# A selective-scan loop in another layout: one state on 128 channels a unit in place of four states on 32 channels

## The chip, the cores and the metric

The kernel runs on one core of one Trainium2 chip. The metric is the device time of one execution in microseconds (us). In the profile the engines are PE (TensorE matmuls), PEld (TensorE weight loads), DVE (VectorE), ACT (ScalarE), POOL (GpSimd) and SP (SyncE, which only issues transfers here). Each engine works through its own queue in order; a semaphore wait at the head of a queue holds back everything behind it.

## The reference

Four images of 192 x 64 x 64 pass through four layers, all in f32. Only the first two matter here:

- Layer 0: a layer norm over the 192 channels, then two Mamba blocks side by side (the second sees the channels reversed), and `xs + y1 + y2`.
- Layer 1: a layer norm, one Mamba block, a 3x3 depthwise convolution with batch norm and gelu, another layer norm, and an MLP of 768 hidden channels.
- Layers 2 and 3: a dynamic 3x3 convolution and a sedenion (16-component) window product with an MLP.

The core of a Mamba block, for 384 inner channels d, 16 states n and 4,096 positions t:

```
dt = softplus(dt @ dt_w.T + dt_b)
A  = -exp(A_log)
h[d,n] = exp(dt[d] * A[d,n]) * h[d,n] + (dt[d] * x[d]) * B[n]     # along t
y[d]   = sum over n of h[d,n] * C[n]   + D[d] * x[d]
y = y * silu(z)
```

So for every pair (d, n) there is a first-order recurrence along 4,096 positions, with a factor, an input and a weighted sum over n around it.

## The kernel before, in words

The program is three stages, one after the other: `two_mambas` (layer 0), `mamba_block` (layer 1) and `conv_and_windows` (layers 2 and 3, not touched). The last one starts when the first two have ended.

A Mamba block is traced by two pieces. `Mamba.front` (L240) makes the inputs of the scan for 512 positions (T): projection, a causal convolution as matmuls with diagonal matrices, silu, the small projection to B, C and dt (`dbl`), softplus of dt, and `dtx = dt*xc`. It writes dt, dtx, xc, z and B/C to DRAM (`keep`). I call one Mamba block on one tile of 512 positions a round: 64 rounds in layer 0 (4 images x 8 tiles x 2 blocks), 32 in layer 1.

The class `Scan` (L321) then works in units. A unit is a tile of 128 partitions that hold 32 channels x 4 states, and 1,024 elements a partition: in layer 0 one group of channels on 1,024 positions (P = 1, S = 4 units make 128 channels), in layer 1 two groups on 512 positions (P = 2, S = 2). There are 2,304 units. For each:

- `load` (L344), six units ahead: dt and dtx come from DRAM with each channel's row repeated on four partitions (L354), B and C with four rows repeated for 32 channels (L359), on SP's queue;
- `inputs` (L365), two units ahead: `w = dtx * B` on POOL (L369), into a pool of S + 3 buffers;
- `decay` (L373), one unit ahead: `dA = exp(dt * A)` on ACT, written to PSUM (L376), 2 buffers;
- `run` (L381): the scan on DVE (L388), in place in dA, or into w in one unit of four; ACT saves the last column as the state (L396); `w = h * C` on DVE reading PSUM, or in that one unit of four on POOL (L398);
- `add_up` (L400): when the S units of 128 channels are done, PE sums over states. Each matmul multiplies by a 128 x 32 selection matrix (`sel`) and writes 32 of the 128 output partitions of ps_y (L420). The skip term `D*x` is a matmul with a diagonal matrix into the same sum (L407);
- `gate` (L429): `y = ps_y * z` on DVE, reading PSUM (L433).

`Scan.stream` writes this order out by hand. Between units it takes steps of the `Background` queue (one a unit in layer 0, two in layer 1), in which the next tile's `front` and the work behind the last tile (`back`, `tail`) are cut up by `yield`. In these generators a matmul stands one step ahead of the ACT instruction that reads its result. A scheduler of the framework then fixes each engine's order when the program is built; it stays close to this one. An f32 matmul appears in the profile as two PE records.

Of the kernel before, what the change touches and what calls it, by code (L numbers as in the profile page):

```python
# [33 lines left out]
NJ = DI // 32  # L34
NQ = NS // 4
UW = 1024
# [172 lines left out]
class Mamba:  # L209
# [3 lines left out]
    def __init__(self, nc, name, taps, ins, const, work, psum, ident):  # L213
        self.nc, self.name, self.taps = nc, name, taps
        self.work, self.psum = work, psum
# [8 lines left out]
        self.conv_b, self.dt_b = w["conv_b"], w["dt_b"]  # L224
        self.x_w, self.out_w = w["x_w"], w["out_w"]
        self.A = const.tile([128, NQ, NJ], F32, name=f"{name}_A")
# [3 lines left out]
        self.D = const.tile([128, ND, 128], F32, name=f"{name}_D")  # L230
        for d in range(ND):
            for j in range(taps):
                nc.vector.tensor_scalar_mul(
                    self.conv[:, d, j, :], ident, w["conv_w"][:, d, j : j + 1]
                )
            nc.vector.tensor_scalar_mul(self.D[:, d, :], ident, w["D"][:, d : d + 1])
        self.halo = const.tile([128, ND, taps - 1], F32, name=f"{name}_halo")
        self.state = const.tile([128, NQ, NJ], F32, name=f"{name}_state")

    def front(self, xn, first, kept, at):  # L240

        nc, K = self.nc, self.taps
        cols = slice(at, at + T)

        def keep(name, t):
            nc.sync.dma_start(kept[name].rearrange("(d p) t -> p d t", p=128)[:, :, cols], t)

        raw = self.work.tile([128, ND, K - 1 + T], F32, name="raw", tag="raw", bufs=1)
        if first:
            nc.gpsimd.memset(raw[:, :, 0 : K - 1], 0.0)  # L250
        else:
            nc.gpsimd.tensor_copy(raw[:, :, 0 : K - 1], self.halo)
        z = self.work.tile([128, ND, T], F32, name="z", bufs=1)

        def project(e):
            ps = self.psum.tile([128, T], F32, name="ps_in", tag="mm")
            for k in range(2):
                nc.tensor.matmul(  # L258
                    ps, self.in_w[:, k, bass.ts(e, 128)], xn[:, k, :], start=(k == 0), stop=(k == 1)
                )  # L260
            return ps

        ps = project(0)
        for e in range(2 * ND):
            after = project(e + 1) if e + 1 < 2 * ND else None
            yield
            nc.scalar.copy(raw[:, e, K - 1 :] if e < ND else z[:, e - ND, :], ps)
            ps = after
        nc.gpsimd.tensor_copy(self.halo, raw[:, :, T:])
        xc = self.work.tile([128, ND, T], F32, name="xc", bufs=1)  # L270

        def convolve(d):
# [5 lines left out]
            return ps  # L278

        ps = convolve(0)  # L280
        for d in range(ND):
            after = convolve(d + 1) if d + 1 < ND else None
            yield
            nc.scalar.activation(xc[:, d, :], ps, AF.Identity, bias=self.conv_b[:, d : d + 1])  # L284
            ps = after
        nc.scalar.activation(xc, xc, AF.Silu)
        nc.scalar.activation(z, z, AF.Silu)
        keep("xc", xc)
        keep("z", z)
        yield  # L290
        ps = self.psum.tile([RK + 2 * NS, T], F32, name="ps_x", tag="mm")
        for d in range(ND):
            nc.tensor.matmul(ps, self.x_w[:, d, :], xc[:, d, :], start=(d == 0), stop=(d == ND - 1))
        yield
        dbl = self.work.tile([RK + 2 * NS, T], F32, name="dbl", bufs=1)
        nc.scalar.copy(dbl, ps)
        nc.sync.dma_start(kept["bc"][:, cols], dbl[RK:, :])
        dt = self.work.tile([128, ND, T], F32, name="dt", bufs=1)
        dtx = self.work.tile([128, ND, K - 1 + T], F32, name="dtx", tag="raw", bufs=1)[:, :, 0:T]

        def step_size(d):
            ps = self.psum.tile([128, T], F32, name="ps_dt", tag="mm")
            nc.tensor.matmul(ps, self.dt_w[:, bass.ts(d, 128)], dbl[:RK, :], start=True, stop=True)
            return ps

        ps, after = step_size(0), step_size(1)
        yield
        for d in range(ND):
            nc.scalar.activation(dt[:, d, :], ps, AF.Softplus, bias=self.dt_b[:, d : d + 1])  # L309
            ps, after = after, step_size(d + 2) if d + 2 < ND else None  # L310
        keep("dt", dt)
        yield
        for d in range(ND):
            nc.gpsimd.tensor_tensor(dtx[:, d, :], dt[:, d, :], xc[:, d, :], ALU.mult)
            if d < ND - 1:
                yield
        keep("dtx", dtx)
        yield


class Scan:  # L321

    AHEAD = 6

    def __init__(self, nc, ts, const, work, dram, psum_a, psum_y, ident):
        self.nc, self.ts, self.P, self.S = nc, ts, UW // ts, 4 * ts // UW  # L330
        self.work, self.dram, self.psum_a, self.psum_y = work, dram, psum_a, psum_y
        self.sel = const.tile([128, 32], F32, name="sel")
        nc.vector.tensor_reduce(
            self.sel, ident.rearrange("p (m n) -> p m n", n=4), AX.X, ALU.add
        )

    def block(self, mamba, first):
        kept = {
            n: self.dram.tile([rows, self.ts], F32, name=f"k_{n}")
            for n, rows in (("dt", DI), ("dtx", DI), ("xc", DI), ("z", DI), ("bc", 2 * NS))  # L340
        }
        return {"m": mamba, "first": first, "kept": kept, "used": {}}

    def load(self, u):  # L344
        nc, ts, P, S = self.nc, self.ts, self.P, self.S
        blk, c, q, s = u
        kept, used = blk["kept"], blk["used"]
        if q == 0:
            for n in ("dt", "dtx"):
                t = used[n, c, s] = self.work.tile([128, P, ts], F32, name=f"u_{n}", bufs=S + 1)  # L350
                for p in range(P):
                    j = 4 * c + s * P + p
                    rows = kept[n][bass.ts(j, 32), :]
                    nc.sync.dma_start(t[:, p, :], rows.unsqueeze(1).broadcast_to([32, 4, ts]))  # L354
        if s == 0:
            for n, r in (("B", 0), ("C", NS)):
                t = used[n, c, q] = self.work.tile([128, ts], F32, name=f"u_{n}", bufs=P + 1)
                rows = kept["bc"][r + 4 * q : r + 4 * q + 4, :]
                nc.sync.dma_start(t, rows.unsqueeze(0).broadcast_to([32, 4, ts]))  # L359
        if s == S - 1 and q in (0, 1):  # L360
            n = ("xc", "z")[q]
            t = used[n, c] = self.work.tile([128, ts], F32, name=f"u_{n}", bufs=1)
            nc.sync.dma_start(t, kept[n][bass.ts(c, 128), :])

    def inputs(self, u):  # L365
        blk, c, q, s = u
        blk["w", c, q, s] = w = self.work.tile([128, self.P, self.ts], F32, name="w", bufs=self.S + 3)
        b = blk["used"]["B", c, q].unsqueeze(1).broadcast_to([128, self.P, self.ts])
        self.nc.gpsimd.tensor_tensor(w, blk["used"]["dtx", c, s], b, ALU.mult)  # L369

    def decay(self, u):
        blk, c, q, s = u
        a = blk["a", c, q, s] = self.psum_a.tile([128, self.P, self.ts], F32, name="dA")  # L373
        for p in range(self.P):
            j = 4 * c + s * self.P + p
            self.nc.scalar.activation(  # L376
                a[:, p, :], blk["used"]["dt", c, s][:, p, :], AF.Exp, scale=blk["m"].A[:, q, j : j + 1]
            )

    def run(self, u, on_pool):  # L380
        nc, P = self.nc, self.P  # L381
        blk, c, q, s = u
        a, w = blk.pop(("a", c, q, s)), blk["w", c, q, s]
        h = w if on_pool else a
        j = 4 * c + s * P
        state = blk["m"].state[:, q, j : j + P]
        for p in range(P):
            nc.vector.tensor_tensor_scan(  # L388
                h[:, p, :],
                a[:, p, :],  # L390
                w[:, p, :],
                0.0 if blk["first"] else state[:, p : p + 1],
                ALU.mult,
                ALU.add,
            )
        nc.scalar.copy(state, h[:, :, self.ts - 1])  # L396
        cc = blk["used"]["C", c, q].unsqueeze(1).broadcast_to([128, P, self.ts])
        (nc.gpsimd if on_pool else nc.vector).tensor_tensor(w, h, cc, ALU.mult)  # L398

    def add_up(self, u):  # L400

        nc = self.nc
        blk, c, q, _ = u
        if q == 0:
            y = blk["ps", c] = self.psum_y.tile([128, self.ts], F32, name="ps_y")
            for f in range(0, self.ts, T):
                nc.tensor.matmul(  # L407
                    y[:, f : f + T],
                    blk["m"].D[:, c, :],
                    blk["used"]["xc", c][:, f : f + T],  # L410
                    start=True,
                    stop=False,
# [642 lines left out]
```

## Time and profile before

| what | value |
|---|---|
| median of 3 runs | 14730.03 us (14729.88 to 14732.33) |
| the profiled execution's own time | 14730.03 us |
| its span, first to last instruction | 14728.2 us |
| layer 0, to its last output addition | 0 to 6830 us |
| start of layer 1 | 6830 to 6930 us |
| layer 1, to its last gate | 6930 to 11184 us |
| what is left of layer 1 | 11184 to 11324 us |
| layers 2 and 3 | 11324 to 14728 us |
| PE / DVE / ACT / POOL busy over the span | 77% / 59% / 44% / 49% |
| moved by DMA | 1757.87 MB |

The page of the profile has a row for each group of instructions: line, engine, operation, result <- operands, partitions x elements, count | busy time, mean ns of one | idle time of the engine just before them and what ended it. A view by stretches gives each engine's busy time between two moments; a view of waits lists who waited for whom. "Busy" of PE is modelled, since matmuls are pipelined.

### The profile page before, as it was taken

How to read it: one execution, taken by the hardware profiler on the slowest of the kernel's cores; microseconds unless marked ns; L12 is line 12 of the kernel's file. 1: busy time of each engine (PE TensorE's matmuls, PEld its weight loads, DVE VectorE, ACT ScalarE, POOL GpSimd, SP SyncE). 2: the span in 40 equal slices, each digit the busy share in tenths (PEclk: the TensorE clock that was granted, in tenths of full speed). 3: DMA queues.
4: the chain of work that ended last, by engine and by line, in shares of the span. 5: the costliest groups of instructions: out<-in, count | busy, mean ns of one | idle time of the engine just before them, and what ended most of it. 6: DMA issues, size and time to landing. Idle time of an engine off the chain costs nothing. (4 is left out here: it accounts for less than half of the span.)

```text
span 14728.2 us, 102888 instructions
## 1 busy us (share of the span) xinstructions
PE 11322.9 (77%) x33872; PEld 4780.0 (32%) x33872; DVE 8669.0 (59%) x6906; ACT 6445.1 (44%) x9214; POOL 7256.2 (49%) x3526
## 2 busy tenths in 40 slices
PE   6676666667766666675788888888885897979799
PEld 2221222222212222222233333333332564646465
DVE  5778877777688877776766666666664203030210
ACT  4455544445455544454555555565552111111111
POOL 5677767777677766775655555555552000000000
PEclk8787777778777777787888888888887898989899
DMA  4445544555455544544443443443442000000000
GB/s 158 158 169 177 172 160 164 171 173 176 153 176 176 169 166 160 178 170 146 148 135 125 141 135 127 138 135 128 137 134 56 11 5 11 5 13 5 5 3 7
DMA packets 758081, 1757.87 MB, mean 119 GB/s; under 512 B 115060, under 2 KB 148120, under 8 KB 757448
## 3 DMA queue, kind: packets, MB, share of 16 engines
q1 hardware_dynamic: 756784, 1748.13, 36.2%
q8 instruction: 266, 4.36, 0.1%
q10 hardware_dynamic: 760, 3.16, 0.1%
q14 instruction: 271, 2.22, 0.0%
HBM read 1405.00 MB, written 346.03 MB: 119 GB/s over the span
## 5 line engine op out<-in xcount | busy, mean ns | idle before, releaser
L369 POOL TENSOR_TENSOR w<-u_dtx,u_B 128x1024 f32<-128x1024 f32 x2304 | 5351.1, 2350 | 2499.2 <-PE ps_y L420 2157.9
L420 PE MATMUL ps_y<-w,sel 128*32 128x512 f32 x9216 | 2616.8, 757 | 1954.1 <-POOL w L398 1303.9
L388 DVE TENSOR_TENSOR_SCAN dA<-dA,m_state,w 128x512 f32<-128x512 f32 (+1 forms) x1872 | 3281.8, 1772 | 970.3 <-ACT m_state L396 570.5
L376 ACT ACTIVATE dA<-u_dt,m_A 128x1024 f32<-128x1024 f32 (+1 forms) x3072 | 2758.3, 902 | 1040.3 <-DVE w L398 818.7
L398 DVE TENSOR_TENSOR w<-dA,u_C 128x1024 f32<-128x1024 f32 x1728 | 2060.1, 1210 | 456.2 <-ACT m_state L396 455.7
L398 POOL TENSOR_TENSOR w<-w,u_C 128x1024 f32<-128x1024 f32 x576 | 1352.0, 2347 | 622.6 <-ACT m_state L396 622.6
L420 PEld LDWEIGHTS ps_y<-w,sel 128*32 128x32 f32 x9216 | 412.9, 121 | 3757.4 <-POOL w L398 1677.0
L388 DVE TENSOR_TENSOR_SCAN w<-dA,m_state,w 128x512 f32<-128x512 f32 (+1 forms) x624 | 1087.1, 1759 | 254.3 <-POOL w L369 156.3
L396 ACT COPY m_state<-dA 128x1 f32<-128x1 f32 (+1 forms) x1728 | 271.3, 157 | 2065.6 <-DVE dA L388 2062.1
L275 PE MATMUL ps_conv<-raw,m_conv 128*128 128x512 f32 x2112 | 1041.7, 636 | 55.9 <-ACT xc L284 55.9
L388 DVE TENSOR_TENSOR_SCAN dA<-dA,w 128x1024 f32<-128x1024 f32 (+1 forms) x432 | 824.7, 1931 | 409.1 <-POOL w L369 160.0
L841 PE MATMUL plus<-xn,t 96*96 96x256 f32 x4352 | 1013.2, 380 | 0.0
L852 DVE TENSOR_TENSOR y<-plus,neg 96x512 f32<-96x512 f32 x64 | 44.0, 687 | 1599.6 <-ACT neg L851 1599.6
L841 PE MATMUL minus<-xn,t 96*96 96x256 f32 x3840 | 939.2, 397 | 11.8 <-ACT xn L171 11.7
L258 PE MATMUL ps_in<-xT,m_in_w 96*128 96x512 f32 x1536 | 858.5, 696 | 60.5 <-ACT dt L309 41.5
L779 POOL MEMSET img<- 96x132 f32 x4 | 0.8, 204 | 1798.0 <-DVE xw L826 1798.0
L841 PEld LDWEIGHTS plus<-xn,t 96*96 96x96 f32 x4352 | 710.0, 163 | 337.7 <-issue 133.1
L189 PE MATMUL ps_h<-xn,t 96*128 96x512 f32 x1536 | 761.6, 641 | 63.0 <-ACT xn L171 60.7
L198 PE MATMUL ps_o<-hid,t 128*96 128x512 f32 x1536 | 739.9, 642 | 36.8 <-ACT hid L194 36.8
L841 PEld LDWEIGHTS minus<-xn,t 96*96 96x96 f32 x3840 | 648.6, 171 | 254.2 <-ACT xn L171 29.0
L376 ACT ACT_TABLE_LOAD x527 | 676.1, 1283 | 9.4
L407 PE MATMUL ps_y<-u_xc,m_D 128*128 128x512 f32 x576 | 393.7, 803 | 350.8 <-DVE m_y L433 345.0
(121 smaller groups left out, 11493.0 us busy)
## 6 DMA issues: line engine op xcount, KB each, us to landing
u_B<-k_bc SPq DMA_DIRECT2D x384, 512.0 KB, 3.9
u_C<-k_bc SPq DMA_DIRECT2D x384, 512.0 KB, 4.1
u_dt<-k_dt SPq DMA_DIRECT2D x384, 512.0 KB, 5.9
u_dtx<-k_dtx SPq DMA_DIRECT2D x384, 512.0 KB, 4.6
u_B<-k_bc SPq DMA_DIRECT2D x384, 256.0 KB, 3.1
u_C<-k_bc SPq DMA_DIRECT2D x384, 256.0 KB, 3.1
u_dt<-k_dt SPq DMA_DIRECT2D x384, 256.0 KB, 3.8
u_dtx<-k_dtx SPq DMA_DIRECT2D x384, 256.0 KB, 3.3
```

Source lines behind the costliest of these rows:

```text
L189: nc.tensor.matmul(ps, self.w1[:, k, bass.ts(m, 128)], x[:, k, :], start=(k == 0), stop=(k == 1))
L198: nc.tensor.matmul(ps, self.w2[:, m, bass.ts(k, CP)], h[:, m, :], start=(m == 0), stop=(m == NH - 1),)
L258: nc.tensor.matmul(ps, self.in_w[:, k, bass.ts(e, 128)], xn[:, k, :], start=(k == 0), stop=(k == 1))
L275: nc.tensor.matmul(ps, self.conv[:, d, j, :], raw[:, d, j : j + T], start=(j == 0), stop=(j == K - 1))
L369: self.nc.gpsimd.tensor_tensor(w, blk["used"]["dtx", c, s], b, ALU.mult)
L376: self.nc.scalar.activation(a[:, p, :], blk["used"]["dt", c, s][:, p, :], AF.Exp, scale=blk["m"].A[:, q, j : j + 1])
L388: nc.vector.tensor_tensor_scan(h[:, p, :], a[:, p, :], w[:, p, :], 0.0 if blk["first"] else state[:, p : p + 1], ALU.mult, ALU.add,)
L396: nc.scalar.copy(state, h[:, :, self.ts - 1])
L398: (nc.gpsimd if on_pool else nc.vector).tensor_tensor(w, h, cc, ALU.mult)
L407: nc.tensor.matmul(y[:, f : f + T], blk["m"].D[:, c, :], blk["used"]["xc", c][:, f : f + T], start=True, stop=False, skip_group_check=True,)
L420: nc.tensor.matmul(y[32 * g : 32 * g + 32, f : f + T], self.sel, ws[s][:, p, f : f + T], start=False, stop=q == NQ - 1, skip_group_check=True,
L841: nc.tensor.matmul(ps[:, m, :], w["sed"][:, cc, s ^ k, bass.ts(m, CP)], xn[:, cc, bass.ts(s, NWIN)], start=(n == 0 and cc == 0), stop=(n = ...
```

## The change

It touches `Mamba`, `two_mambas` and `mamba_block`; the class `Scan` goes. A unit is now one state n of 128 channels on 512 positions: 48 units a round (16 states x 3 groups of 128 channels, the group running fastest), 4,608 in all. dt, dtx, xc and z stay in SBUF; only B and C (`bc`) go through DRAM, and come back two states at a time, repeated on all 128 partitions. A matmul and the ACT instruction that reads it now stand in the same background step. One background step is taken a unit, and at the end of a round the background is drained. Softplus is written out as max(x,0) + ln(1+exp(-|x|)) with a correction term. The skip term is a DVE instruction that reads the sum, and the gate a POOL instruction.

```diff
 def front(self, xn, first, u):
...
+        for d in range(ND):
+            ps = self.psum.tile([128, T], F32, name="ps_dt", tag="mm")
+            nc.tensor.matmul(ps, self.dt_w[:, bass.ts(d, 128)], dbl[:RK, :], start=True, stop=True)
+            nc.scalar.activation(dt[:, d, :], ps, AF.Identity, bias=self.dt_b[:, d : d + 1])
+        yield
+        e = self.work.tile([128, ND, T], F32, name="sp_e", bufs=1)
+        nc.scalar.activation(e, dt, AF.Abs)
+        nc.scalar.activation(e, e, AF.Exp, scale=-1.0)
+        dtx = u["dtx"] = self.work.tile([128, ND, T], F32, name="dtx", bufs=2)
+        nc.gpsimd.tensor_scalar(dtx, e, 1.0, 1.0, ALU.add, ALU.subtract)
+        nc.gpsimd.tensor_tensor(dtx, e, dtx, ALU.subtract)
+        nc.scalar.activation(e, e, AF.Ln, bias=1.0)
+        yield
+        nc.vector.scalar_tensor_tensor(dt, dt, 0.0, e, ALU.max, ALU.add)
+        nc.gpsimd.tensor_tensor(dt, dt, dtx, ALU.add)
+        nc.gpsimd.tensor_tensor(dtx, dt, xc, ALU.mult)
+        yield
-            nc.scalar.activation(dt[:, d, :], ps, AF.Softplus, bias=self.dt_b[:, d : d + 1])
-        keep("dt", dt)
-        for d in range(ND):
-            nc.gpsimd.tensor_tensor(dtx[:, d, :], dt[:, d, :], xc[:, d, :], ALU.mult)
-        keep("dtx", dtx)
+    def scan(self, u, first, background):
+        if first:
+            nc.vector.memset(self.state, 0.0)
+        dt, dtx, bc = u["dt"], u["dtx"], u["bc"]
+        ys = [self.psum_y.tile([128, T], F32, name=f"y{d}") for d in range(ND)]
+        def add_up():
+            d, n, w = late.popleft()
+            nc.tensor.matmul(ys[d], self.ident, w, start=(n == 0), stop=(n == NS - 1))
+        def load(n0):
+            for name, r in (("Bs", n0), ("Cs", NS + n0)):
+                t = self.work.tile([128, NG, T], F32, name=name, bufs=2)
+                nc.sync.dma_start(t, bc[r : r + NG, :].unsqueeze(0).broadcast_to([128, NG, T]))
+        def inputs(n, d):
+            if n % NG == 0 and d == 0:
+                load(n)
+            w = ws[n, d] = self.work.tile([128, T], F32, name="w", bufs=6)
+            nc.gpsimd.tensor_tensor(w, dtx[:, d, :], pairs[n - n % NG][0][:, n % NG, :], ALU.mult)
+        def decay(n, d):
+            dA = dAs[n, d] = self.psum_a.tile([128, T], F32, name="dA")
+            nc.scalar.activation(dA, dt[:, d, :], AF.Exp, scale=self.A[:, d, n : n + 1])
...
+        for i, (n, d) in enumerate(units):
+            if i + 2 < len(units):
+                inputs(*units[i + 2])
+            if i + 1 < len(units):
+                decay(*units[i + 1])
+            on_pool = i % 4 == 3
+            h = w if on_pool else dA
+            nc.vector.tensor_tensor_scan(h, dA, w, st, ALU.mult, ALU.add)
+            nc.scalar.copy(st, h[:, T - 1 : T])
+            engine = nc.gpsimd if on_pool else nc.vector
+            engine.tensor_tensor(w, h, pairs[n - n % NG][1][:, n % NG, :], ALU.mult)
+            late.append((d, n, w))
+            if len(late) > 2:
+                add_up()
+            background.step()
+        while late:
+            add_up()
+        background.drain()
+        for d in range(ND):
+            nc.vector.scalar_tensor_tensor(
+                y[:, d, :], xc[:, d, :], self.D[:, d : d + 1], ys[d], ALU.mult, ALU.add
+            )
+        nc.gpsimd.tensor_tensor(y, y, z, ALU.mult)
...
-        psum_a = ctx.enter_context(tc.tile_pool(name="l0_a", bufs=2, space=PSUM))
+        psum_a = ctx.enter_context(tc.tile_pool(name="l0_a", bufs=3, space=PSUM))
...
         for n, u in enumerate(units):
+            background.add(front(u, 1))
+            mambas[0].scan(u[0], u["t"] == 0, background)
+            background.add(front(after, 0))
+            mambas[1].scan(u[1], u["t"] == 0, background)
+            background.add(back(u))
...
-        psum_y = ctx.enter_context(tc.tile_pool(name="l1_y", bufs=2, space=PSUM))
-        psum_a = ctx.enter_context(tc.tile_pool(name="l1_a", bufs=2, space=PSUM))
+        psum_y = ctx.enter_context(tc.tile_pool(name="l1_y", bufs=1, space=PSUM))
+        psum_a = ctx.enter_context(tc.tile_pool(name="l1_a", bufs=3, space=PSUM))
...
         for n, u in enumerate(units):
+            load(units[n + 1])
+            background.add(front(units[n + 1]))
+            mamba.scan(u["m"], u["t"] == 0, background)
+            background.add(back(u))
+            background.add(tail(u["b"], u["t"] - 1))
```

## The prediction

> **What bounds the kernel now.** I read first the busy times by stretches, with cuts where layer 0 ends, layer 1 starts, scans its last unit and drains:
>
> ```profile
> core 0: us, PE busy (x) PEld busy (x) DVE busy (x) ACT busy (x) POOL busy (x), PEclk, DMA share, GB/s
> 0.00:6830.00 6830.00, 4624.21 (x12160) 1449.60 (x12160) 5185.57 (x3365) 3334.64 (x4707) 4819.34 (x2312) 0.78 0.49 167
> 6830.00:6930.00 100.00, 74.19 (x176) 31.88 (x180) 36.87 (x63) 46.91 (x69) 30.79 (x22) 0.74 0.47 154
> 6930.00:11184.00 4254.00, 3524.08 (x9457) 1307.02 (x9449) 2795.56 (x2488) 2468.59 (x3753) 2398.16 (x1174) 0.82 0.42 134
> 11184.00:11324.00 140.00, 106.83 (x228) 45.28 (x228) 9.74 (x14) 31.06 (x33) 5.60 (x9) 0.77 0.02 6
> 11324.00:14728.00 3404.00, 2993.60 (x11856) 1946.24 (x11856) 641.22 (x976) 563.93 (x653) 2.35 (x10) 0.90 0.05 9
> ```
>
> No engine is full in the two scan stages. Layer 0 takes 6830/64 = 106.7 us a round: DVE 81.0 (76%), POOL 75.3 (71%), PE 72.3 (68%). Layer 1 takes 4254/32 = 132.9: PE 110.1 (83%), DVE 87.4 (66%), ACT 77.1, POOL 74.9. The stages are held by waits between in-order queues around a loaded DVE, and in layer 1 also PE. The view of waits says which:
>
> ```profile
> POOL w L369 <- PE ps_y L420: 2157.9, 443, 17.4
> ...
> DVE dA L388 <- ACT m_state L396: 709.8, 247, 8.1
> ...
> DVE w L398 <- ACT m_state L396: 455.7, 252, 7.6
> ...
> DVE dA L388 <- POOL w L369: 422.4, 119, 75.8
> ```
>
> POOL mostly waits for w buffers that PE gives back only with the sum of a whole group. DVE waits for ACT (each C product waits for the state copy) and for B products. The durations come from the groups with shapes kept apart:
>
> ```profile
> L388 DVE TENSOR_TENSOR_SCAN dA<-dA,m_state,w 128x1024 f32<-128x1024 f32 x864 | 2006.8, 2346 | 634.0 <-ACT m_state L396 416.3 <-POOL w L369 145.0 <-ACT dA L376 52.4
> L388 DVE TENSOR_TENSOR_SCAN dA<-dA,m_state,w 128x512 f32<-128x512 f32 x1008 | 1275.1, 1280 | 336.2 <-ACT m_state L396 154.1 <-POOL w L369 117.3 <-ACT dA L376 49.9
> L376 ACT ACTIVATE dA<-u_dt,m_A 128x512 f32<-128x512 f32 x1536 | 1051.8, 689 | 485.0 <-DVE w L398 451.7 <-DVE w L388 7.7 <-DMA u_dt<-k_dt 7.5
> L314 POOL TENSOR_TENSOR dtx<-dt,xc 128x512 f32<-128x512 f32 x288 | 361.0, 1268 | 350.0 <-ACT dt L309 348.6 <-ACT m_state L396 1.3
> L433 DVE TENSOR_TENSOR m_y<-ps_y,u_z 128x512 f32<-128x512 f32 x96 | 65.2, 679 | 56.7 <-PE ps_y L420 55.2
> ```
>
> These price a 512-element scan, decay, POOL product and PSUM product. Two timeline lines of PE price the sums:
>
> ```profile
> 4205.41 1.92 PE L420 MATMUL ps_y<-w,sel 128*32 128x512 f32 x16
> ```
>
> ```profile
> 9027.91 5.32 PE L275 MATMUL ps_conv<-raw,m_conv 128*128 128x512 f32 x12
> ```
>
> A full-width record goes by in 5.32/12 = 0.44 us, a 32-wide one in 1.92/16 = 0.12 us.
>
> **What the Trainium skill says.** TensorE: Matmul & The Clock Gate, Part 3, section "The mechanism": matmuls on different tiles of the array run at the same time; the 0.12 against 0.44 us above agrees. The same page, Part 1, section "What's actually happening": PE runs at half clock until it has been busy for a window of about 3.4 us; the granted 0.78 and 0.82 fit such a mix. GPSIMD Engine Reference, section "3.1 Elementwise — side-by-side cycle accounting": a two-input operation costs about 2.6 cycles an element, a one-input one at best 1.8 in a plain loop; for the first the trace has (2350-1268)/512 = 2.11 ns (1024 against 512 elements), for the second no large row. ScalarE: Activation LUTs, section "What ACT_TABLE_LOAD costs": 1283 ns; the trace has exactly that (L376's loads, 527, mean 1283).
>
> **The change, part by part**, per round.
>
> Scan and C product on DVE. 48 scans of about 1.28 (12 of them into w, 1.27) = 61.3 us; 36 C products x 0.68 = 24.5. Before, the same elements cost 24 x 2.3 (layer 0) and 18 x 1.21. Skip term: 3 PSUM reads at about 0.74 (L694's mean) = 2.2. The max-add of softplus, 1536 elements: 1218 ns at 1024 and 679 at 512 extend to 1.76. The gates go. Norm and output work stays: 294.6/64 = 4.6 (layer 0); norms, image and MLP additions 8.1 (layer 1). Sum: 94.4 us (was 81.0) and 97.9 (was 87.4).
>
> POOL. 60 products x 1.268 = 76.1. Softplus correction, dt, dtx and gate: four two-input operations of 1536 at 2.11 ns + 0.19 = 3.43 each, 13.7; one one-input operation of 1536, between 1.8 and 3.4, taken 2.5 (an estimate, 1.8 cycles an element at the page's 1.2 GHz). Norm 1.8, or the residual 2.4; halo 0.4. Sum about 94.5 and 95.1 (was 75). The dtx products (3.8) go.
>
> ACT. 48 decays x 0.689 + 48 copies x 0.165 = 41.0, against 34.7 in layer 0 (24 x 1.116 + 48 x 0.165, its copies counted at most so high). Three more passes of 1536 (Abs, Exp, Ln) at 1.484 = 4.5. The built programs hold 1141 table loads before and 893 after: 248 x 1.283/96 = 3.3 us less a round. ACT comes to about 66 and 87: not the bound, but Ln and both silus still block it about 4 us each (load, 1.48, load), and every C product waits for a copy in that queue.
>
> PE. 48 sums are 96 records on both sides, but now 128 wide: 96 x (0.44-0.12) = +31, less the skip matmuls, 6 x 0.44: +28 us at full clock, double that at half clock. My count at full clock: 72 in layer 0 and 117 in layer 1 (158 other records of 512, 48 short ones). At the clocks granted now that is 92 and 143.
>
> DMA. 1,536 loads of 512 KB for B and C = 805 MB replace most of 1,748 MB. I cost this at nothing: each is issued when its buffer frees, six units (some 11 us) before use, and lands in about 4. On SP's queue a B or C load waits behind the other one's buffer, the bc store (for ACT) and the x and output transfers; those waits have the same 11 us as cover. Without it each of 8 pairs a round would add up to 4 us. The dt, dtx, xc and z transfers go; nothing waited long for them (DMA waits of POOL and DVE in the list are at most 142 us).
>
> New waits. A round's last C product is on POOL; behind it stand PE's last sum, the skip terms on DVE, then the POOL gate of 3.4 us. DVE has one or two units of the next round queued between; after that next B products wait. I put 2 us a round on this, about the 2.3 us (220.9/96) of the gates' wait now, so no net cost. The background drain costs nothing: layer 0 has 19 steps, layer 1 34 (one tile in eight 49), in 48 units.
>
> Where the stall goes. Six w buffers, given back one by one, remove the group wait of POOL. But DVE and POOL are now loaded alike, POOL can run only two or three units (of 1.8 us) ahead because each POOL C product waits for its scan, and the 1.28 us scan that covers a state copy was 2.35 us in layer 0. ACT's evictions again follow their matmul in the same step, so they wait on a busier PE. I see no reason for DVE to be better used than now, and take the same shares: 94.4/0.759 = 124.4 us x 64 = 7960; 97.9/0.657 = 149.0 x 32 = 4768 (PE's 117 to 143 fits beneath that). With the 100 + 140 + 3404 that stay: 16372, plus 1.8 us outside the span (14730.03 - 14728.2; that execution is the median) = 16374, so 16,370 us.
>
> **The rivals.**
> - *Buffers free, faster.* The group wait was what held all engines; DVE's share rises to 0.87. For: 2157.9 us of POOL waits on PE, the longest row; shorter units, no DMA round trip. Against: DVE itself waited only 422.4 + 186.1 us for B products. DVE needs 64 x 94.4 + 32 x 97.9 = 9175 us; 9175/0.87 + 3646 = 14,192. It decides from 9175/11084 = 0.828: above that share the kernel is faster, and now it is 7981/11084 = 0.72.
> - *Balanced.* Part of this: share 0.80, 9175/0.80 + 3646 = 15,115. Against it: four loaded queues.
> - *PE becomes the bound of layer 1.* Spread sums keep the clock low: 143 us at PE's present share of 0.83 = 172 x 32 = 5504; with 7960 in layer 0: 17,110. For: layer 1 has PE as its fullest engine. Against: a PE that full should be granted more clock.
>
> **How the numbers follow.** Forecast 0.50; PE bound 0.25; balanced 0.15; faster 0.08; within 0.2% of no change 0.02 (0.2% is about what a measurement of this kernel can tell from none). That makes slower 0.90. The range runs from the balanced case, 15,050, to 17,450 (PE bound with some 170 us in layer 0 for the unknown POOL operation and cold sums); it leaves out the faster case and what lies beyond. All slower cases together are the range itself.
>
> **What would show it.** In the profile after: scans near 1.28 us x 4608, DVE C products near 0.68 x 3456, POOL products near 1.27 x 5760, POOL operations of 1536 near 3.4; DVE and POOL both about 94 us a round busy; PE records of the sum 0.44 us apart or more; rounds of 124 and 149 us; DVE waiting for ACT and B products. I am wrong if DVE's share in the stages is above 0.80, if the 512-wide operations are dearer than their rows here, or if PE is over 90% busy in layer 1.

## The result, and the profile after

The changed kernel takes 16361.12 us (median of 4 runs, 16333.99 to 16366.56) against 14731.18 for the kernel before (14729.88 to 14733.64): ratio 1.1103, 95% interval 1.1083 to 1.1122. It is slower by 1,630 us. The forecast was 16,370. The profiled execution has a span of 16357.0 us.

First the busy times by stretches, with the cuts where the forecast put them (layer 0, start of layer 1, layer 1 to its last gate, its drain, layers 2 and 3):

```profile
core 0: us, PE busy (x) PEld busy (x) DVE busy (x) ACT busy (x) POOL busy (x), PEclk, DMA share, GB/s
0.00:7740.00 7740.00, 5717.03 (x11776) 2366.25 (x11776) 5622.59 (x6214) 3938.16 (x7833) 6174.77 (x4369) 0.85 0.22 74
7740.00:7840.00 100.00, 68.99 (x151) 31.92 (x152) 29.88 (x58) 44.18 (x65) 35.67 (x28) 0.71 0.23 70
7840.00:12807.00 4967.00, 4031.81 (x9278) 1642.25 (x9276) 2899.21 (x3102) 2554.92 (x4511) 3034.46 (x2195) 0.88 0.18 59
12807.00:12953.00 146.00, 109.18 (x236) 46.51 (x236) 9.72 (x14) 31.07 (x33) 9.15 (x10) 0.79 0.03 8
12953.00:16357.00 3404.00, 2995.74 (x11856) 1948.77 (x11856) 641.34 (x976) 564.03 (x653) 2.28 (x9) 0.90 0.05 9
```

A round takes 7740/64 = 120.9 us in layer 0 (106.7 before) and 4967/32 = 155.2 in layer 1 (132.9 before). So layer 0 lost 910 us and layer 1 713; everything else is where it was. The fullest engine of layer 0 is now POOL (6174.77/7740 = 80%, before 71%); DVE fell from 76% to 73%. In layer 1 PE has 81% and no other engine more than 61%.

The groups of the scan loop and of softplus (busy time, mean ns of one, idle time just before them):

```profile
L319 POOL TENSOR_TENSOR w<-dtx,Bs 128x512 f32<-128x512 f32 x4608 | 5831.7, 1286 | 1997.5 <-PE y L304 1984.3
...
L337 DVE TENSOR_TENSOR_SCAN dA<-dA,m_state,w 128x512 f32<-128x512 f32 x3456 | 4352.2, 1280 | 2327.0 <-POOL w L319 1993.7 <-ACT xc L263 307.1 <-issue 15.4
...
L340 DVE TENSOR_TENSOR w<-dA,Cs 128x512 f32<-128x512 f32 x3456 | 2252.0, 676 | 204.6 <-ACT m_state L338 203.5
...
L285 POOL TENSOR_SCALAR dtx<-sp_e 128x1536 f32<-128x1536 f32 x96 | 516.6, 5382 | 74.0 <-ACT sp_e L283 74.0
...
L290 POOL TENSOR_TENSOR dt<-dt,dtx 128x1536 f32<-128x1536 f32 x96 | 329.0, 3428 | 92.3 <-DVE dt L289 92.3
...
L289 DVE SCALAR_TENSOR_TENSOR dt<-dt,sp_e 128x1536 f32<-128x1536 f32 x96 | 284.8, 2967 | 74.5 <-ACT sp_e L287 74.5
```

Scan, C product and B product cost what the rows of before said. One operation on POOL does not cost what the forecast took: L285, the first step of softplus's correction, takes 5.38 us. The waits have turned round. Before, over both layers, DVE lost 709.8 + 455.7 us to ACT's state copies and 422.4 to B products. Now, by the view of waits of layer 0 alone (0 to 7740 us; total us, times, longest):

```profile
PE y L304 <- POOL w L340: 1293.4, 395, 13.3
DVE dA L337 <- POOL w L319: 1083.9, 489, 8.5
...
POOL w L319 <- PE y L304: 839.8, 689, 5.0
...
POOL w L340 <- ACT m_state L338: 457.3, 192, 4.7
```

and of layer 1 alone:

```profile
POOL w L319 <- PE y L304: 1144.6, 340, 22.3
DVE dA L337 <- POOL w L319: 901.4, 252, 13.3
```

The largest of these waits form a circle: DVE waits for a B product from POOL, POOL waits for a w buffer that a sum on PE frees, PE waits for a C product from POOL. The timeline shows where the circle is cut in layer 0:

```profile
4005.19 3.41 POOL L290 TENSOR_TENSOR dt<-dt,dtx 128x1536 f32<-128x1536 f32 x1
...
4008.68 3.42 POOL L291 TENSOR_TENSOR dtx<-dt,xc 128x1536 f32<-128x1536 f32 x1
...
4012.06 1.26 POOL L340 TENSOR_TENSOR w<-w,Cs 128x512 f32<-128x512 f32 x1
4013.28 3.72 POOL L319 TENSOR_TENSOR w<-dtx,Bs 128x512 f32<-128x512 f32 x3
4013.38 0.50 PEld L304 LDWEIGHTS y<-w,ident 128*128 128x128 f32 x2 [7.80 <-POOL w L340]
...
4014.58 1.28 DVE L337 TENSOR_TENSOR_SCAN w<-dA,m_state,w 128x512 f32<-128x512 f32 x1 [4.60 <-POOL w L319]
```

The last softplus operation and the dtx product behind it (3.41 + 3.42 us) hold POOL's queue. The C product behind them starts at 4012.06, PE's sums stand for 7.80 us, and DVE, with its two units ahead used up, stands for 4.60 us until the B products come. In layer 1 the cut is on PE instead, here at the start of a round:

```profile
9980.20 7.12 PE L529 MATMUL ps_out<-m_y,m_pack 128*96 128x512 f32 x12 [3.64 <-POOL m_y L354]
...
9987.16 7.89 PE L553 MATMUL ps_dw<-img,dw 96*96 96x512 f32 x18
...
9994.89 1.02 PE L304 MATMUL y<-w,ident 128*128 128x512 f32 x2
...
9995.75 7.89 PE L553 MATMUL ps_dw<-img,dw 96*96 96x512 f32 x18
...
9995.99 1.26 POOL L319 TENSOR_TENSOR w<-dtx,Bs 128x512 f32<-128x512 f32 x1 [12.18 <-PE y L304]
...
10003.48 4.46 PE L304 MATMUL y<-w,ident 128*128 128x512 f32 x10
...
10004.58 3.73 POOL L319 TENSOR_TENSOR w<-dtx,Bs 128x512 f32<-128x512 f32 x3 [4.44 <-PE y L304]
...
10005.89 3.75 DVE L337 TENSOR_TENSOR_SCAN dA<-dA,m_state,w 128x512 f32<-128x512 f32 x3 [7.31 <-POOL w L319]
```

PE, which has waited 3.64 us for POOL's gate of the round before, runs the output matmuls and eighteen depthwise records (7.12 + 7.89 us). Only then come two records of sums; POOL, without a free w buffer until they have run, has idled 12.18 us. Eighteen more records go ahead of the next ten of sums: POOL idles 4.44 us, and DVE behind it 7.31. The 307.1 us that the scans' row puts down to ACT are 23 waits of layer 1. The one that ends at 8176.89 us (13.35 us long) is of the same kind: PE ran 24 records of the projection and 18 of the convolution (11.03 + 7.89 us) ahead of the sums, and the scan's B product was not made before 8176.86.

### The profile page after: what moved, and what is told of

Same layout as the page of the kernel before. It is cut to its first block, busy times and chain, and to the rows that moved or that the text cites. A ratio compares the mean times of both kernels' runs of the same rounds, so it can differ in the third digit from the quotient of the medians.

```text
span 16357.0 us, 107534 instructions
## 1 busy us (share of the span) xinstructions
PE 12922.7 (79%) x33296; PEld 6035.7 (37%) x33296; DVE 9202.7 (56%) x10363; ACT 7132.4 (44%) x13094; POOL 9256.3 (57%) x6610
## 2 busy tenths in 40 slices
DMA packets 328043, 902.39 MB, mean 55 GB/s; under 512 B 78196, under 2 KB 111256, under 8 KB 327368
## 4 chain that ended last, share of the span: by engine, by line
PE 41%; POOL 32%; DVE 10%; issue 9%; ACT 7%; DMA 0%; DVEq 0%; POOLq 0%; SPq 0%; ACTq 0%
POOL w L319 16%; PE y L304 8%; PE plus L703 6%; PE minus L703 5%; POOL w L340 5%; PE ps_conv L258 4%; PE ps_h L187 4%; DVE dA L337 3%; POOL dtx L285 3%; PE ps_dw L553 3%; PE ps_o L196 2%; PE ps_in L248 2%; POOL dt L290 2%; POOL dtx L286 2%; POOL m_y L354 2%
## 5 line engine op out<-in xcount | busy, mean ns | idle before, releaser
L304 PE MATMUL y<-w,ident 128*128 128x512 f32 x9216 | 5245.2, 703 | 2272.2 <-POOL w L340 1806.9
L319 POOL TENSOR_TENSOR w<-dtx,Bs 128x512 f32<-128x512 f32 x4608 | 5831.7, 1286 | 1997.5 <-PE y L304 1984.3
L337 DVE TENSOR_TENSOR_SCAN dA<-dA,m_state,w 128x512 f32<-128x512 f32 x3456 | 4352.2, 1280 | 2327.0 <-POOL w L319 1993.7
L304 PEld LDWEIGHTS y<-w,ident 128*128 128x128 f32 x9216 | 1924.9, 221 | 5246.4 <-POOL w L340 2334.1
L323 ACT ACTIVATE dA<-dt,m_A 128x512 f32<-128x512 f32 x4608 | 3071.3, 685 | 1219.1 <-DVE w L340 1132.0
L340 DVE TENSOR_TENSOR w<-dA,Cs 128x512 f32<-128x512 f32 x3456 | 2252.0, 676 | 204.6 <-ACT m_state L338 203.5
L340 POOL TENSOR_TENSOR w<-w,Cs 128x512 f32<-128x512 f32 x1152 | 1460.4, 1268 | 763.8 <-ACT m_state L338 763.4
L337 DVE TENSOR_TENSOR_SCAN w<-dA,m_state,w 128x512 f32<-128x512 f32 x1152 | 1464.0, 1271 | 681.5 <-POOL w L319 521.5
L338 ACT COPY m_state<-dA 128x1 f32<-128x1 f32 x3456 | 540.6, 158 | 2599.9 <-DVE dA L337 2594.6
L258 PEld LDWEIGHTS ps_conv<-raw,m_conv 128*128 128x128 f32 x2112 | 410.3, 194 | 541.4 <-issue 524.4
```

Of the source, the lines that this page charges most:

```text
L258: nc.tensor.matmul(ps, self.conv[:, d, j, :], raw[:, d, j : j + T], start=(j == 0), stop=(j == K - 1))
L304: nc.tensor.matmul(ys[d], self.ident, w, start=(n == 0), stop=(n == NS - 1))
L319: nc.gpsimd.tensor_tensor(w, dtx[:, d, :], pairs[n - n % NG][0][:, n % NG, :], ALU.mult)
L323: nc.scalar.activation(dA, dt[:, d, :], AF.Exp, scale=self.A[:, d, n : n + 1])
L337: nc.vector.tensor_tensor_scan(h, dA, w, st, ALU.mult, ALU.add)
L338: nc.scalar.copy(st, h[:, T - 1 : T])
```

## The experiments

The theories after reading the trace: *load*, the queues of POOL and DVE have too much work for the two units of distance, POOL above all; and *hold*, the six w buffers come back too late because the sums stand behind other work on PE. Each was timed beside the kernel before on the same chip; the median of before was 14735.67 to 14737.7 us there. The differences from after are taken from its 16361.12 us. The table gives, for each kernel, its time, its ratio to before, and, from the busy times by stretches, the round of each layer and POOL's busy time and share in layer 0. The stretches are cut at each kernel's own last output addition and last gate, so a last digit can differ from the one above.

| kernel | us | ratio (95%) | round, layer 0 / 1 | POOL a round, layer 0 |
|---|---|---|---|---|
| before | 14731 | 1 | 106.7 / 133.0 | 75.3 (71%) |
| after | 16361 | 1.110 (1.108 to 1.112) | 120.9 / 155.3 | 96.5 (80%) |
| a_softplus | 15069 | 1.0225 (1.021 to 1.024) | 106.5 / 144.0 | 83.2 (78%) |
| a_nocorr | 15120 | 1.0261 (1.0246 to 1.0276) | 106.7 / 145.1 | 84.7 (79%) |
| a_chop | 16383 | 1.1121 (1.1103 to 1.114) | 120.3 / 157.4 | 96.7 (80%) |
| a_halfsum | 15274 | 1.0363 (1.0347 to 1.0378) | 112.5 / 138.2 | 96.5 (86%) |
| a_w8 | 16031 | 1.088 (1.0861 to 1.0898) | 119.7 / 148.1 | 96.0 (80%) |
| a_cdve | 15871 | 1.077 (1.0754 to 1.0786) | 115.3 / 151.5 | 82.2 (71%) |
| a_sp_w11 | 14865 | 1.009 (1.0075 to 1.0105) | 104.8 / 140.9 | 83.2 (79%) |
| a_sp_w11_shift | 14823 | 1.0058 (1.0041 to 1.0075) | 105.0 / 139.4 | 83.1 (79%) |
| a_sp_w11_late | 14956 | 1.0148 (1.0133 to 1.0163) | 106.3 / 140.6 | 83.2 (78%) |
| a_gate10 | 14557 | 0.9875 (0.9859 to 0.9892) | 104.5 / 131.9 | 79.9 (76%) |
| b_wide | 14790 | 1.0038 (1.0023 to 1.0053) | 108.3 / 131.7 | 75.4 (70%) |
| b_softhand | 15177 | 1.0297 (1.0282 to 1.0312) | 113.1 / 134.1 | 87.8 (78%) |

**a_softplus: the written-out softplus undone.**

```diff
-            nc.scalar.activation(dt[:, d, :], ps, AF.Identity, ...)
+            nc.scalar.activation(dt[:, d, :], ps, AF.Softplus, ...)
-        nc.scalar.activation(e, dt, AF.Abs)
...
-        nc.gpsimd.tensor_scalar(dtx, e, 1.0, 1.0, ALU.add, ALU.subtract)
-        nc.gpsimd.tensor_tensor(dtx, e, dtx, ALU.subtract)
-        nc.scalar.activation(e, e, AF.Ln, bias=1.0)
-        yield
-        nc.vector.scalar_tensor_tensor(dt, dt, 0.0, e, ALU.max, ALU.add)
-        nc.gpsimd.tensor_tensor(dt, dt, dtx, ALU.add)
```

> The changed kernel with the softplus of the kernel before (one ACT function in place of Abs, Exp, Ln, three GpSimd operations and one VectorE operation of 1536 elements). It takes 516.6 + 328.5 + 329.0 = 1174 us off GpSimd, 285 off VectorE and 426 off ACT, and brings back table loads. Theory L (two equally loaded queues, VectorE and GpSimd, each held up by what the other has on top): 800 to 1174 us faster than 16361, so 15190 to 15560. Theory H (the w buffers, held by the 128-wide TensorE sums, hold GpSimd's B products, and these the scans): GpSimd's load hardly matters, 16000 to 16300.

Measured 15068.56 us, 1,293 less than after. That is faster than either range, below the one of load (15190 to 15560). In layer 0, POOL's work fell by 96.5 - 83.2 = 13.3 us a round and the round by 14.4, all that layer 0 had lost; in layer 1 the round fell by 11.3, half of its loss. Undoing the softplus takes back four fifths of the whole loss.

**a_halfsum: half the sums.** The sums over odd states are left out, so y lacks half of its terms.

```diff
-            nc.tensor.matmul(ys[d], self.ident, w, start=(n == 0), stop=(n == NS - 1))
+            if n % 2 == 0:
+                nc.tensor.matmul(ys[d], self.ident, w, start=(n == 0), stop=(n == NS - 2))
```

> The changed kernel with the TensorE sum of every odd state left out, so the output lacks half of the sum over states; nothing else is changed. TensorE loses 2304 sums of 0.88 us, 2028 us, and half of the w buffers no longer wait for it. Theory H: most of GpSimd's 1984 us of waits for the sums go, 14900 to 15500. Theory L: GpSimd and VectorE have the same work, 16000 to 16361.

Measured 15273.67 us, 1,087 less. The round lost 17.1 us in layer 1 and 8.4 in layer 0, and POOL's wait for sums fell from 1,984 to 704.9 us. That is in the range of hold. POOL now reaches 86% in layer 0, the highest share of all these kernels: with less of the hold it comes nearer to its own work. The edit takes work off PE and lets buffers go sooner, both at once; it can't tell these two apart.

**a_w8: 8 w buffers in place of 6.**

```diff
-            w = ws[n, d] = self.work.tile([128, T], F32, name="w", bufs=6)
+            w = ws[n, d] = self.work.tile([128, T], F32, name="w", bufs=8)
```

> The changed kernel with 8 w buffers in place of 6. Theory H: two units more of slack (some 4 us) against waits of 1984 us in 1029 pieces; 500 to 1000 us faster, 15360 to 15860. Theory L: 0 to 300 us faster, 16060 to 16361.

Measured 16031.49 us, 330 less, between the two ranges: 7.2 us a round in layer 1, 1.2 in layer 0. Two more buffers help in layer 1 and nearly not in layer 0, where half the sums had still taken 8.4 us off a round.

**b_wide: the kernel before with sums as wide as those of after.** The selection matrix is padded with zeros to 128 columns; each sum writes all 128 partitions.

```diff
-                    y[32 * g : 32 * g + 32, f : f + T],
-                    self.sel,
+                    y[:, f : f + T],
+                    self.sel[:, g, :],
...
```

> The kernel before with one part of the change alone: the sums over states as 128-wide matmuls (the selection matrix padded with zeros to 128 columns, all 128 partitions of the sum written each time), as many matmuls as before. My count is +31 us of TensorE a round at full clock, 2950 us in all, beside a fullest engine of 83% in layer 1. Theory H: 600 to 1200 us slower than 14731, 15330 to 15930, most of it in layer 1. Theory L: TensorE has room, 0 to 300 us slower.

Measured 14790.07 us, only 53 more than the kernel before beside it. PE's busy time over the span rises to 85% (77% before), but its granted clock rises from 0.82 to 0.907, and the round of layer 1 is even 1.3 us shorter. My term of +28 us of PE work a round is thus no cost by itself in the old loop.

**a_nocorr: only the correction's three POOL operations left out** (dt lacks a small term); the ScalarE passes, their table loads and the max-add stay.

```diff
-        nc.gpsimd.tensor_scalar(dtx, e, 1.0, 1.0, ALU.add, ALU.subtract)
-        nc.gpsimd.tensor_tensor(dtx, e, dtx, ALU.subtract)
...
-        nc.gpsimd.tensor_tensor(dt, dt, dtx, ALU.add)
```

> The kernel after, with the correction term of softplus left out (three of the four GpSimd operations of softplus: 5.4 + 3.4 + 3.4 us a round), so its dt lacks a small term; the three ScalarE passes, their table loads and the max-add on VectorE stay. Theory amount (GpSimd's work): the 1,293 us that the one-instruction softplus saved come nearly all from these operations, 12.2 us x 96 = 1,170 us of GpSimd: 15,150 to 15,400. Rival ScalarE (its passes and table loads, which hold decays and state copies): 15,950 to 16,250.

Measured 15119.86 us, 1,241 less than after, just past the range of the theory of amount. Of the 1,293 us of a_softplus, ScalarE's three passes with their table loads and DVE's max-add are worth 51 together. In layer 1, too, these three POOL operations count: without them POOL has 10.5 us less a round, and the round is 10.2 shorter, though POOL had only 61% there. The rival (ScalarE) falls.

**a_chop: the same POOL operations in pieces of 512**, each in a background step of its own.

```diff
+        for d in range(ND):
+            nc.gpsimd.tensor_scalar(dtx[:, d, :], e[:, d, :], 1.0, 1.0, ALU.add, ALU.subtract)
+            yield
+            nc.gpsimd.tensor_tensor(dtx[:, d, :], e[:, d, :], dtx[:, d, :], ALU.subtract)
+            yield
...
```

> The kernel after, with each 1,536-wide GpSimd operation of softplus (the two of the correction, the addition to dt, dtx) cut into three of 512 in background steps of their own; the same work, some 1.9 us more of fixed cost a round. Theory amount (what counts is how much GpSimd has to do): 16,300 to 16,500. Rival clump (the blocks of 5.4 + 3.4 and 3.4 + 3.4 us, behind which the next B products stand, empty VectorE's queue): 15,700 to 16,000, and VectorE's wait for B products falls from 2,515 us to under 1,900.

Measured 16383.22 us, 22 more than after. DVE's wait of its scans into dA for B products stays at 2035.2 us (1993.7 after). The long blocks catch the eye in the timeline above, but cutting them gains nothing: it is the amount that costs.

**a_cdve: all C products on DVE.**

```diff
-            on_pool = i % 4 == 3
+            on_pool = False
```

> The kernel after, with all C products on VectorE and all scans in PSUM: VectorE +12 x 0.68 = 8 us a round, GpSimd -15 us. Theory amount (GpSimd's queue): 14,950 to 15,500, VectorE's share in the scan stages above 0.80. Rival VectorE (its work sets the pace, 8 us a round at its present shares): 17,300. Rival hold (w buffers are held by the sums, whoever makes the product): 16,000 to 16,300.

Measured 15870.98 us, 490 less than after; none of the three ranges has it. In layer 0 POOL's work fell by 14.3 us a round, a little more than in a_softplus, but the round by only 5.6, while DVE went up to 93.9 us (81% of the round). The waits say what was late next:

```profile
POOL w L319 <- PE y L304: 3314.1, 1332, 23.5
...
DVE dA L337 <- POOL w L319: 1778.0, 551, 16.9
```

POOL now waits for sums far more (1984.3 after). So this edit took POOL's work away and made the hold worse and DVE fuller at once; how much each of these cost was not measured.

**a_sp_w11: one-instruction softplus and 11 w buffers** (the edit of a_softplus, and `bufs=11`).

> The kernel after, with the one-instruction softplus of the kernel before and 11 w buffers in place of 6. Alone the first gave -1,293 us and 8 buffers -330. If the two are separate costs: 14,450 to 14,750. If the wait for w buffers that is left after the first is what holds it (2,218 us of GpSimd waits for sums): below 14,450. If the buffers only mattered because GpSimd was late: 14,950 to 15,070.

Measured 14865.17 us, 203 below a_softplus, between the ranges: more than if buffers had mattered only because POOL was late, less than separate costs. POOL's wait for sums fell from 2218.4 to 1214.5 us; 3.1 us a round were won in layer 1, 1.7 in layer 0.

**b_softhand: the written-out softplus in the kernel before.** The three dtx products also become one, with two background steps fewer.

```diff
-            nc.scalar.activation(dt[:, d, :], ps, AF.Softplus, ...)
+            nc.scalar.activation(dt[:, d, :], ps, AF.Identity, ...)
...
+        nc.gpsimd.tensor_scalar(dtx, e, 1.0, 1.0, ALU.add, ALU.subtract)
+        nc.gpsimd.tensor_tensor(dtx, e, dtx, ALU.subtract)
...
+        nc.gpsimd.tensor_tensor(dt, dt, dtx, ALU.add)
```

> The kernel before with softplus written out as in the kernel after: the same four GpSimd operations of 1,536 (17 us with dtx, in place of 3.8), three ScalarE passes and the max-add, in the old scan loop. Theory room (the price is high in the kernel after because its GpSimd is full; before, GpSimd has 75 of 107 us of work): 14,950 to 15,400. Rival own price (the written-out softplus costs some 1,290 us in any loop): 15,900 to 16,150.

Measured 15176.7 us: +439 in the old loop, against 1,293 in the new one. It adds 12.5 us of POOL a round in layer 0 and 11.9 in layer 1. The old loop, where POOL had 71% in layer 0 and 56% in layer 1, took up half of it in layer 0 (the round grew by 6.4) and nearly all of it in layer 1 (+1.1). The price of the softplus is the price of POOL's time in the loop around it.

**a_sp_w11_shift: the last C product of a round on DVE.**

```diff
-            on_pool = i % 4 == 3
+            on_pool = i % 4 == 1
```

> The kernel after with one-instruction softplus, 11 w buffers, and the C products on GpSimd in units 1, 5, ... 45 of a round in place of 3, 7, ... 47, so that the last product of a round is VectorE's; the same work. Against 14,865 with the products where they were. If the end of a round (the last product on GpSimd, then the sum, the skip term, the gate) costs the 2 us that the forecast put on it: 14,650 to 14,720. If that end is covered: 14,820 to 14,900.

Measured 14822.71 us, 42 less than a_sp_w11: 1.5 us a round in layer 1, nothing in layer 0. This wait at the round's end is nearly covered, or the gain is taken back elsewhere; the run does not tell which.

**a_sp_w11_late: evictions one background step after their matmuls**, as before the change (the projection is shown; the convolution and the small projection go the same way).

```diff
+        ps = project(0)
         for e in range(2 * ND):
+            after = project(e + 1) if e + 1 < 2 * ND else None
+            yield
             nc.scalar.copy(raw[:, e, K - 1 :] if e < ND else z[:, e - ND, :], ps)
-            yield
+            ps = after
...
```

> The kernel after with one-instruction softplus, 11 w buffers, and the evictions of the projection, the convolution and the small projection one background step behind their matmuls, as in the kernel before. Against 14,865 with matmul and eviction in one step. If ScalarE's queue, blocked by evictions that wait for PE, delays decays and state copies: 14,550 to 14,750. If PE is on time: 14,820 to 14,900.

Measured 14956.32 us, 91 more than a_sp_w11, outside both ranges, on the side that neither expected. So there is no sign that evictions waiting for PE held ACT up in a way that this order would mend. Why later evictions cost something was not followed.

**a_gate10: one-instruction softplus, 10 w buffers, C products on POOL in units 1, 5, ..., and the old end of a round.** The diff shows the end of the round alone.

```diff
+            if n == NS - 1:
+                nc.tensor.matmul(ys[d], self.Dd[:, d, :], u["xc"][:, d, :], start=False, stop=False)
...
-            nc.vector.scalar_tensor_tensor(
-                y[:, d, :], xc[:, d, :], self.D[:, d : d + 1], ys[d], ALU.mult, ALU.add
-            )
-        nc.gpsimd.tensor_tensor(y, y, z, ALU.mult)
+            nc.vector.tensor_tensor(y[:, d, :], ys[d], z[:, d, :], ALU.mult)
```

> The new loop with all that helped so far: one-instruction softplus, 10 w buffers (11 no longer fit), C products on GpSimd in units 1, 5, ...; and the end of a round as in the kernel before: the skip term as a matmul with a diagonal matrix, the gate as three VectorE products that read PSUM, no GpSimd gate. Against 14,823: GpSimd -3.4 us a round (329 us in all), PE +2.6 us, VectorE about even. Theory amount (GpSimd's work still sets the pace): 14,480 to 14,650, faster than the kernel before. If GpSimd's amount no longer matters once it is down to 79 us a round: 14,780 to 14,870. If PE's added records count in layer 1: above 14,870.

Measured 14557.03 us (14554.32 to 14559.62): 266 less than a_sp_w11_shift, and faster than the kernel before, ratio 0.9875 (0.9859 to 0.9892). The busy times by stretches of this kernel, layer 0 and layer 1:

```profile
0.00:6691.00 6691.00, 5475.88 (x12143) 2270.33 (x12144) 5328.75 (x6151) 3834.25 (x7769) 5116.29 (x4110) 0.92 0.25 85
6791.00:11012.00 4221.00, 3894.43 (x9456) 1600.22 (x9455) 2809.74 (x3059) 2483.20 (x4464) 2533.52 (x2064) 0.96 0.21 69
```

The total lies in the range of the theory of amount, but the place does not fit it: 3.4 us of POOL a round should have shown in both layers, and the round fell by 0.5 us in layer 0 and by 7.5 in layer 1. In layer 1 two rows of a_sp_w11_shift's waits change. PE's output matmuls (L519) waited 107.8 us for the POOL gate, with everything queued behind them, and now wait 65.8 for the DVE gate. DVE waited for those matmuls:

```profile
DVE img L526 <- PE ps_out L519: 320.3, 33, 35.4
```

and in a_gate10:

```profile
DVE img L527 <- PE ps_out L520: 106.3, 5, 34.2
```

A gate that ends sooner lets PE go on sooner; that fits the place, but gate and skip term were not tried apart, so it is argued and not shown. Against a_sp_w11_shift, one w buffer less went in with them. Nor was the old loop tried with this kernel's gains, where such exist.

## Why the prediction was right, and where two errors cancelled

The direction and the time came out, and the list of work was good; the division of the time between the layers and the engine that sets it were not.

- *Work.* Scans 1280 and 1271 ns (1.28 and 1.27 forecast), C products 676 (0.68), B products 1286 (1.268). POOL came to 96.5 and 94.8 us a round (94.5 and 95.1), ACT to 61.5 and 79.8 (66 and 87). The 66 and 87 don't follow from the forecast's own terms: these, added to ACT's busy time before (52.1 and 77.1), give about 60 and 78.
- *L285.* I took 2.5 us, an estimate after the Trainium skill's GPSIMD Engine Reference, section "3.1 Elementwise — side-by-side cycle accounting" (1.8 cycles an element at best), between bounds of my own, 1.8 and 3.4. It measured 5.38, outside both ends: the upper bound, that an operation with one input is no dearer than one with two, was wrong for this one, which does two arithmetic steps. The +2.9 us a round were partly balanced by my other POOL terms.
- *DVE.* Forecast 94.4 and 97.9 us a round; the busy time by stretches has 87.9 and 90.6. Most of the gap is a slip of method: I divided a sum of single durations by a share that came from the busy view, where records that overlap count once. The single durations of layer 0 add up to 5933 us, 92.7 a round, near the forecast; the busy time is 5623. With one measure throughout (before: 5332.5 us of durations in 6830 us, 78.1%), the same step would have given 94.4/0.781 = 120.9 us for layer 0, which is what it took. That exact match is luck, as the next point shows. Two terms differed within the sum: L399 took 530 ns in place of 1487, L289 2967 in place of 1760. Both contain waits for POOL, as the last section shows.
- *Same shares.* "I see no reason for DVE to be better used than now, and take the same shares." By busy time DVE's share was 0.759 and is 0.726 in layer 0, and 0.657 against 0.584 in layer 1. So rounds came to 120.9 us (forecast 124.4) and 155.2 (149.0): -220 us in layer 0, +199 in layer 1. The median was right because these cancel.
- *What sets layer 0.* The forecast scaled DVE's work. By that reckoning, undoing the softplus takes 1.76 us of DVE off a round, which makes 1.76/0.759 x 64 + 1.76/0.657 x 32 = 234 us in all; it took off 1,293. The runs show POOL's work: with a_softplus and a_nocorr, 13.3 and 11.8 us less POOL work made the round 14.4 and 14.2 shorter, while DVE's work fell by only 3.3 and 1.3. POOL's share stays at 78% to 80% in after, a_softplus, a_nocorr, a_chop, a_w8 and a_sp_w11, and b_softhand ends at 78% too. It goes higher only when half the sums are gone (86%), so the 80% is no limit of POOL but belongs to this loop with its sums; and it is lower in a_cdve (71%) and a_gate10 (76%). In a_softplus, a_nocorr and a_sp_w11 DVE is as full as POOL (79% to 81%), so there POOL's share alone names no bound, and 3.2 us less POOL work in a_gate10 gained only 0.5 in layer 0. That POOL sets layer 0 of after rests on a_softplus and a_nocorr. My text named "DVE and POOL now loaded alike" as the reason for not expecting more; it should have made POOL's 94.5 us over a share of its own a second sum beside DVE's. With the share before (71%) that gives 134 us, too much; the 80% was learnt only from these runs.
- *What sets layer 1.* Two steps failed here. The first is "PE's 117 to 143 fits beneath that". PE came to 4031.81/32 = 126 us at a clock of 0.88, fitting beneath 149 as an amount. But its order did not fit: long runs of background matmuls stand ahead of the sums, six buffers don't last over them, and a_halfsum, a_w8 and a_gate10 all gain most a round there. The second is the end of a round, put at no net cost: the old end gained a_gate10 7.5 us a round in layer 1, with the doubt on its parts said above. But POOL's work counts in layer 1 as well: a_softplus gained 11.3 us a round, half of what layer 1 had lost. The chain of work that ended last passes through L285 for 3.3% of layer 1 in after, about 164 us of the 166.9 that L285 takes there. The rival that came nearest in place, PE as the bound of layer 1 at 172 us a round, named the engine and missed the way it acts: PE is 81% busy in that stage.
- *PE's clock.* The rival's "spread sums keep the clock low" is refuted: the clock rose from 0.78 and 0.82 to 0.85 and 0.88. That more activity gets more clock is what the Trainium skill says, TensorE: Matmul & The Clock Gate, Part 1, section "What's actually happening". Layer 0 agrees (PE busy 68% before, 74% after), and so does b_wide (77% to 85% over the span, clock 0.82 to 0.907). Layer 1 does not by this measure: PE's busy share fell from 83% to 81% while the clock rose.
- *Waits.* "DVE waiting for ACT and B products" was half right: B products, 1993.7 + 521.5 us; the wait of C products for the state copy fell to 203.5 (455.7 before). The wait of the skip term for the last sums, put at 2 us a round, is 238.8/96 = 2.5; what the end of a round costs beyond that wait is said under layer 1.
- *DMA.* Costed at nothing, rightly: 902.39 MB moved (1757.87 before), and no wait for Bs or Cs among the large rows of the waits.
- *"Buffers free, faster"* needed DVE above 0.828. Releasing buffers one by one did not release POOL: its wait for sums only went from 2157.9 us to 1984.3.

## What to carry to other kernels

When a change loads a second engine, make a sum for each of them, its work over the share that it can reach in such a loop, in the same measure, and take the larger result: in layer 0 here POOL, not DVE. The price of an operation moved onto an engine depends on the loop around it: the same softplus cost 439 us in one loop and 1,293 in the other. How full the engine is does not settle it. In layer 1, about 12 us of POOL work cost 1.1 us a round in the old loop, where POOL had 56%, and 11.3 in the new one, where POOL without it has 58%. Where buffers come back through an in-order engine, look at the longest run of other work that can stand ahead of the release, not at the engine's busy share.

## What the runs showed of the hardware that was not expected

- A POOL operation with one input and two arithmetic steps (add, then subtract) on 128x1536 f32 took 5382 ns, 3.50 ns an element, and 5379 in b_softhand; one with two inputs and one step took 3428 ns. Whether the second step is the cause was not measured.
- Sums that write 128 partitions in place of 32 raised PE's granted clock from 0.82 to 0.907 in b_wide and cost 0.4% of the time.
- Two DVE instructions and POOL's took turns. L289, the max-add of softplus, took 1740 to 5275 ns within one run of after:

```profile
L289 DVE SCALAR_TENSOR_TENSOR dt<-dt,sp_e x96: 1740/2828/5275, 77.2 to 12674.3; 128x1536 f32<-128x1536 f32 x96
```

The 28 that start while POOL runs nothing take 1740 to 1759 ns. The 68 that start during a POOL instruction take 2514 to 5275, and every one of them ends 1.61 to 1.62 us after a POOL instruction has ended. POOL is held up in turn: the B product that started at 4001.17 us, during one of them, took 2.83 us in place of 1.27. L399's operation on 128x192 shows the same: it took 530 ns on average in after and 1487 in before, but where POOL ran nothing at its start a median of 369 and 372 ns. So the forecast's 1.76 us for L289 was right for the operation alone. This was read from the traces; no run varied it by itself. The scans, which read dA from PSUM, show no such spread (L337: 1250 to 1294 ns over all of them in after).
